# Selective scans on one core: diagonals of B read back from DRAM, softplus terms added by DMAs, the rate product made once

## The chip, the cores and the metric

The kernel runs on one core of a Trainium2 chip. A core has five engines, each with its own instruction stream: TensorE (PE in the profile, its weight loads PEld), VectorE (DVE), ScalarE (ACT), GpSimd (POOL) and SyncE (SP). SP, ACT and POOL can issue transfers (DMAs); all of them run on the core's 16 DMA engines. An engine executes its own stream in order. Engines wait for each other on semaphores, and an instruction that waits holds everything behind it on its engine.

The metric is the device time in microseconds of one execution. A difference under about 0.2% can't be told from no change for this kernel.

## The reference, cut to what matters

Layer 0 (group norm, triangle-style attention over a 256x256x128 map, residual) and the front of layer 1 (group norm, projection, 3x3 depthwise convolution, SiLU) are not touched by the change. What is touched is the selective scan of layer 1, which runs four times over L = 65,536 tokens: along rows, along columns, and both backwards.

```python
delta = softplus(dts + dt_bias)                    # (4, 256, L); dts is an 8-row product
def step(h, inp):                                  # h: (4, 256, 16), over l = 0..L-1
    d_t, x_t, B_t, C_t = inp
    dA = exp(d_t[..., None] * As)                  # decay of each of 16 states
    h = dA * h + (d_t * x_t)[..., None] * B_t[:, :, None, :]
    y = einsum('bkdn,bkn->bkd', h, C_t)            # sum over the 16 states
    return h, y
```

So for each of 4 directions, 256 channels and 16 states there is a recurrence over 65,536 tokens, with coefficient `exp(delta*A)` and input `delta*x*B`; its result is multiplied by C and summed over the 16 states.

## The kernel before, in words

The program goes through stages one after the other: group statistics, pair norm, attention, convolution, a transposing copy, the scans, the output. The scans take the stretch from about 4,700 to 27,660 us.

**Tiles and order of a scan.** Each direction is cut into 64 blocks of 1,024 tokens, so there are 4 x 64 = 256 blocks. The 256 channels are two halves h of 128 partitions, and there are 16 states m. One pair (m, h) is a step s of a block: s = 2m + h, 32 steps in a block. The order is written out by hand (a manual schedule): `body` goes through the steps, and for each step calls the functions below, some for a later step. A loop body covers 18 blocks.

In step s of a block:

- `recur` (L858): DVE's scan instruction runs the recurrence over 1,024 tokens, from the decay tile `da`, the input tile `mm` in PSUM and the `state`. After h = 1 a short reduce (L863) saves the last column, and POOL multiplies both halves of `hs` by the row of C (L865), two instructions.
- `turn` for step s+1: PE makes the next input `delta*x*B` in a PSUM tile `mm`, token tiles of 128 (8 of them, numbered j). `dxt` holds `delta*x` with tokens on the partitions. Half of the tiles (j = 0 to 3, DJ = 4) are a matrix product of `dxt` with a diagonal matrix `dg` whose diagonal is B (L846); each such product is two PE instructions in the profile. The other half are scaled first (`but`) and then transposed (L848), one PE instruction each. There are two `mm` tiles, and everything that makes a PSUM tile of this kind (turn, rate, turn_rate) takes them in turn.
- `collect_some`: PE adds transposes of finished `hs` tiles to the output in PSUM (L617), up to 10 in a step, less in a few steps (`share`).
- `decay` for step s+4: ACT makes `da` = exp(delta*A) (L839).
- `scale` for step s+6: ACT makes the diagonals `dg`, each the identity times a column of B (L833), and the scaled tiles `but` (L835), two of each in a step.
- `fetch` (L826), after h = 1: SP loads the row of C, spread to all partitions (`cc`, 512 KB), for state m+4. Its tile comes free when POOL's multiplications of state m are done, so SP waits there.

In steps 6 and 8 the previous block's output is added to `yb` by DVE (L898), stored, and the next `yb` is loaded in step 16.

**The next block is prepared within the current one.** `begin` returns a list of pieces with a step each and a mark for before or after the scan of that step: (6) and (8) `rate`, an 8-row product plus bias in a `mm` tile (L750), and its absolute value on ACT (L759); (9) exp of minus that; (10) the logarithm of 1 + e (L766); (11) and (12) a rounding remainder w on ACT (L770, L774); (11) to (14) two additions of halves e and w to lw on POOL (L780, L777), so four POOL instructions; (18) and (20) `rate` once more, and `softplus` on DVE (L783), which takes the larger of the rate and zero, and adds lw; (22) and (24) `turn_rate`, which transposes delta on PE (L790), and `times_x` (L794), which multiplies it by x into `dxt` on DVE.

The lines that set the order:

```python
for m in range(4): fetch(blocks[0], m)     # SP, four rows of C ahead
...
recur(B, m, h)                             # DVE (and POOL after h = 1)
do(turn, u + 1)                            # PE
collect_some(...)                          # PE
if nxt: nxt.advance(s, True)               # pieces of the next block
do(decay, u + 4)                           # ACT
do(scale, u + 3 * NH)                      # ACT
if h == NH - 1 and ...: fetch(...)         # SP
```

Of the kernel before, what the change touches and what calls it, by code (L numbers as in the profile page):

```python
# [29 lines left out]
AF = mybir.ActivationFunctionType  # L30
ALU = mybir.AluOpType
# [4 lines left out]
P = 128  # L36
# [4 lines left out]
DI = 256  # L41
# [578 lines left out]
def scans(tc, io, c):  # L620
# [19 lines left out]
    with tc.tile_pool(name="e_w", bufs=1) as wp, tc.tile_pool(name="e_1", bufs=1) as sb1, tc.tile_pool(  # L640
# [14 lines left out]
        DJ = NJ // 2  # L655
# [10 lines left out]
        bus = ring("but", 4, [P, NJ - DJ, DI])  # L666
# [18 lines left out]
        class Block:  # L685
# [43 lines left out]

            def advance(self, now, after):  # L730
                if self.pieces is None:
                    self.pieces = begin(self)
                while self.pieces and self.pieces[0][:2] <= (now, after):
                    _, _, f, *args = self.pieces.pop(0)
                    f(*args)

        def begin(B):
# [20 lines left out]
            def size(h):  # L758
                nc.scalar.activation(B.e[:, h, :], B.pu[h], AF.Abs)  # L759

# [15 lines left out]
            def less(h):  # L776
                nc.gpsimd.tensor_tensor(B.lw[:, h, :], B.lw[:, h, :], B.w[:, h, :], ALU.add)  # L777

            def log1p(h):
                nc.gpsimd.tensor_tensor(B.lw[:, h, :], B.lw[:, h, :], B.e[:, h, :], ALU.add)  # L780

            def softplus(h):
                nc.vector.scalar_tensor_tensor(B.delta[:, h, :], B.pu[h], 0.0, B.lw[:, h, :], ALU.max, ALU.add)  # L783
# [8 lines left out]
            def times_x(i):  # L792
# [8 lines left out]
            return [  # L801
# [6 lines left out]
                (11, True, log1p, 0),  # L808
                (11, True, one_plus),
                (12, True, log1p, 1),  # L810
                (12, True, rest),
                (13, True, less, 0),
                (14, True, less, 1),

                (18, False, rate, 0),
                (18, True, softplus, 0),
                (20, False, rate, 1),
                (20, True, softplus, 1),
# [4 lines left out]
            ]  # L823
# [3 lines left out]

        def scale(B, m, h):  # L830
            dg, bu = dgs[m % 4], bus[m % 4]
            for j in range(h * DJ // 2, (h + 1) * DJ // 2):
                nc.scalar.activation(dg[:, j, :], c.ident, AF.Copy, scale=B.bt[:, B.slot(j), m : m + 1])  # L833
                at = B.slot(DJ + j)
                nc.scalar.activation(bu[:, j, :], B.dxt[:, DJ + j, :], AF.Copy, scale=B.bt[:, at, m : m + 1])  # L835

# [4 lines left out]
        def turn(B, m, h):  # L841
            d1 = B.d1 = mm()
            dg, bu = dgs[m % 4], bus[m % 4]
            hc = slice(h * P, (h + 1) * P)
            for j in range(DJ):
                nc.tensor.matmul(d1[:, j * P : (j + 1) * P], B.dxt[:, j, hc], dg[:, j, :], start=True, stop=True)  # L846
            for j in range(DJ, NJ):
                nc.tensor.transpose(d1[:, j * P : (j + 1) * P], bu[:, j - DJ, hc], c.ident)  # L848
            d1s.append(d1)
# [56 lines left out]
        share = {6: 0, 7: 8, 8: 0, 18: 3, 20: 3, 22: 5, 24: 5}  # L906

        def body(blocks, before, after):
# [16 lines left out]
            if before is None:  # L925
                blocks[0].load()
                blocks[0].load_tokens()
                blocks[0].advance(U, True)
                blocks[0].free = set(range(NJ // PB))
                blocks[1].load()  # L930
                for m in range(4):
                    fetch(blocks[0], m)
                for u in range(3 * NH):
                    do(scale, u)
                for u in range(4):
                    do(decay, u)
                do(turn, 0)
            for x, B in enumerate(blocks):
                nxt = at_hand.get(x + 1)
                for s in range(U):  # L940
# [22 lines left out]
                    do(scale, u + 3 * NH)  # L963
                    if h == NH - 1 and at(u + 1 + 3 * NH):
                        fetch(*at(u + 1 + 3 * NH)[:2])
# [32 lines left out]
def output(tc, io, c):  # L998
# [75 lines left out]
    "y": (NT, DI),  # L1074
}
# [58 lines left out]
```

## Time and profile before

| | |
|---|---|
| time, median of 3 | 28,445.06 us (28,438.65 to 28,445.41) |
| span of the profiled execution | 28,447.5 us |
| PE busy | 26,610.1 us (94%) |
| ACT busy | 25,332.4 us (89%) |
| DVE busy | 24,922.2 us (88%) |
| POOL busy | 22,944.4 us (81%) |
| DMA, mean over the span | 128 GB/s |
| granted TensorE clock, mean | 0.965 |

The profiled execution is given by its span, from its first to its last instruction; it is 2.4 us above the median of the timed runs, under 0.01%.

How it is read: a group line names a line of the kernel, engine, operation, output and inputs, and then busy time, the mean of one instruction, and the idle time of the engine before it with what ended it. A timeline line gives the start in us, how long the merged instructions took, engine, line, operation and count, and in brackets idle time before it and its releaser. A window line gives a stretch, its length, the busy time of PE, PEld, DVE, ACT and POOL (with counts), the granted PE clock (1.00 is full), the DMA engines' busy share and the GB/s. Most of the program is one repeated block, so the block is what has to be read, in order of time.

### The profile page before, as it was taken

How to read it: one execution, taken by the hardware profiler on the slowest of the kernel's cores; microseconds unless marked ns; L12 is line 12 of the kernel's file. 1: busy time of each engine (PE TensorE's matmuls, PEld its weight loads, DVE VectorE, ACT ScalarE, POOL GpSimd, SP SyncE). 2: the span in 40 equal slices, each digit the busy share in tenths (PEclk: the TensorE clock that was granted, in tenths of full speed). 3: DMA queues.
4: the chain of work that ended last, by engine and by line, in shares of the span. 5: the costliest groups of instructions: out<-in, count | busy, mean ns of one | idle time of the engine just before them, and what ended most of it. 6: DMA issues, size and time to landing. Idle time of an engine off the chain costs nothing. (4 is left out here: it accounts for less than half of the span.)

```text
span 28447.5 us, 528099 instructions
## 1 busy us (share of the span) xinstructions
PE 26610.1 (94%) x196490; PEld 22529.2 (79%) x196490; DVE 24922.2 (88%) x24253; ACT 25332.4 (89%) x49673; POOL 22944.4 (81%) x10118
## 2 busy tenths in 40 slices
PE   8999996999999999999999999999999999999998
PEld 3555444888888888888888888888888888888884
DVE  4777665999999999999999999999999999999987
ACT  6875224999999999999999999999999999999987
POOL 2443002999999999999999999999999999999983
PEclk9999998999999999999999999999999999999999
DMA  5112345433433333333334333333333333333335
GB/s 206 55 50 71 111 116 115 132 132 129 133 130 133 132 131 132 132 131 132 128 132 133 131 133 132 131 132 129 132 132 130 133 132 129 132 130 132 133 132 172
DMA packets 1923996, 3630.07 MB, mean 128 GB/s; under 512 B 532297, under 2 KB 1240009, under 8 KB 1889490
## 3 DMA queue, kind: packets, MB, share of 16 engines
q1 hardware_dynamic: 1424722, 3339.77, 34.6%
q10 hardware_dynamic: 496640, 255.88, 3.2%
q8 instruction: 1568, 25.69, 0.4%
q14 instruction: 1066, 8.73, 0.1%
HBM read 3002.42 MB, written 592.84 MB: 126 GB/s over the span
## 5 line engine op out<-in xcount | busy, mean ns | idle before, releaser
L865 POOL TENSOR_TENSOR hs<-hs,cc 128x1024 f32<-128x1024 f32 x8192 | 19202.5, 2380 | 1346.1 <-DVE state L863 679.9
L858 DVE TENSOR_TENSOR_SCAN hs<-da,state,mm 128x1024 f32<-128x1024 f32 x8192 | 18976.6, 2340 | 1465.4 <-PE mm L848 1074.7
L846 PE MATMUL mm<-dg,dxt 128*128 128x128 f32 x65536 | 9305.0, 287 | 1065.1 <-DVE hs L858 886.1
L846 PEld LDWEIGHTS mm<-dg,dxt 128*128 128x128 f32 x65536 | 8328.4, 199 | 2257.9 <-DVE hs L858 1897.8
L839 ACT ACTIVATE da<-delta,A 128x1024 f32<-128x1024 f32 x8192 | 9328.4, 1139 | 112.2 <-PEq L984 76.0
L617 PE MATMUL y<-ident,hs 128*128 128x128 f32 x65536 | 8511.4, 275 | 1.4 <-POOL hs L865 1.4
L835 ACT ACTIVATE but<-dxt,bt 128x256 f32<-128x256 f32 x16384 | 8150.2, 497 | 11.4 <-DVE dxt L794 11.4
L617 PEld LDWEIGHTS y<-ident,hs 128*128 128x128 f32 x65536 | 7494.1, 143 | 1.9 <-POOL hs L865 1.9
L833 ACT ACTIVATE dg<-ident,bt 128x128 f32<-128x128 f32 x16384 | 6393.1, 390 | 0.2
L848 PE MATMUL mm<-ident,but 128*128 128x128 f32 x32768 | 5092.5, 280 | 0.0
L848 PEld LDWEIGHTS mm<-ident,but 128*128 128x128 f32 x32768 | 4011.4, 146 | 0.0
L750 PE MATMUL mm<-dt,dtw 9*128 9x512 f32 x4096 | 2033.0, 615 | 265.9 <-DMA bt<-mid_bk 184.5
L385 POOL TENSOR_TENSOR an<-ex,rs 128x1024 f32<-128x1024 f32 x512 | 970.2, 1895 | 1024.5 <-PE tp L394 566.3
L780 POOL TENSOR_TENSOR lw<-lw,e 128x1024 f32<-128x1024 f32 x512 | 1207.7, 2384 | 336.3 <-ACT lw L766 336.3
L750 PEld LDWEIGHTS mm<-dt,dtw 9*128 9x128 f32 x4096 | 680.7, 184 | 959.5 <-issue 733.3
L500 POOL MEMSET pad<- 128x10 f32 x32 | 3.7, 117 | 1650.0 <-PE ps L537 1639.9
L777 POOL TENSOR_TENSOR lw<-lw,w 128x1024 f32<-128x1024 f32 x512 | 1202.9, 2375 | 0.0
L537 PE MATMUL ps<-pad,w 128*128 128x512 f32 x2048 | 954.8, 610 | 161.0 <-ACT xi L525 161.0
L372 ACT ACTIVATE ex<-sc,nm 128x256 f32<-128x256 f32 x2048 | 1013.7, 499 | 0.4
L759 ACT ACTIVATE e<-mm 128x1024 f32<-128x1024 f32 x512 | 524.7, 1025 | 522.1 <-PE mm L750 521.9
L355 DVE CUSTOM_DVE_ANT_0 sc<-ps,bias 128x256 f32<-128x256 f32 x2048 | 746.2, 421 | 117.3 <-PE ps L340 117.3
L394 PEld LDWEIGHTS tp<-ident,an 128*128 128x128 f32 x4096 | 467.5, 141 | 470.7 <-POOL an L385 235.1
(137 smaller groups left out, 18522.4 us busy)
## 6 DMA issues: line engine op xcount, KB each, us to landing
cc<-mid_dc SPq DMA_DIRECT2D x2048, 512.0 KB
cc<-mid_dcT SPq DMA_DIRECT2D x2048, 512.0 KB
xk<-mid_xk SPq DMA_DIRECT2D x256, 1024.0 KB
yb<-mid_y SPq DMA_DIRECT2D x256, 1024.0 KB
mid_y<-yb SPq DMA_DIRECT2D x256, 1024.0 KB
xt<-mid_xT SPq DMA_DIRECT2D x64, 1024.0 KB
mid_xk<-xk ACTq DMA_DIRECT2D x32, 2048.0 KB
mid_y<-y ACTq DMA_DIRECT2D x32, 2048.0 KB
```

The source lines that it names most:

```text
L372: nc.scalar.activation(exs[u][:, x, :], scs[u][:, e, jt, :], AF.Exp, scale=-1.0, bias=nms[u][:, e, jt : jt + 1], accum_out=sms[u][:, x : x ...
L617: nc.tensor.matmul(out, in_, c.ident, is_transpose=True, start=start, stop=stop, skip_group_check=True)
L750: nc.tensor.matmul(pu[:, q : q + T], dtw[0 : DR + 1, k, h * P : (h + 1) * P], B.dt[0 : DR + 1, q : q + T], start=True, stop=True,)
L777: nc.gpsimd.tensor_tensor(B.lw[:, h, :], B.lw[:, h, :], B.w[:, h, :], ALU.add)
L780: nc.gpsimd.tensor_tensor(B.lw[:, h, :], B.lw[:, h, :], B.e[:, h, :], ALU.add)
L833: nc.scalar.activation(dg[:, j, :], c.ident, AF.Copy, scale=B.bt[:, B.slot(j), m : m + 1])
L835: nc.scalar.activation(bu[:, j, :], B.dxt[:, DJ + j, :], AF.Copy, scale=B.bt[:, at, m : m + 1])
L839: nc.scalar.activation(da, B.delta[:, h, :], AF.Exp, scale=A[:, B.S.k * NH + h, m : m + 1])
L846: nc.tensor.matmul(d1[:, j * P : (j + 1) * P], B.dxt[:, j, hc], dg[:, j, :], start=True, stop=True)
L848: nc.tensor.transpose(d1[:, j * P : (j + 1) * P], bu[:, j - DJ, hc], c.ident)
L858: nc.vector.tensor_tensor_scan(o, d0, d1, state[:, m, h : h + 1], ALU.mult, ALU.add)
L865: nc.gpsimd.tensor_tensor(hs[:, x, :], hs[:, x, :], ccs[m % 4], ALU.mult)
```

## The change

Three edits in the scans; the rest is unchanged.

1. Of eight token tiles three (j = 0, 2, 4) instead of four go through a diagonal. ACT no longer makes the diagonals. Instead, per block, four times (one for each 4 states) ACT copies the columns of B into a zeroed tile `z` with a spacing of 128 (`spread`), SP writes `z` (128 x 1,664, 852 KB) to DRAM, and for each state SP reads back a skewed view of it (`diagonal`, 128 rows of 1,536 bytes, 197 KB): row p starts p elements earlier in its row of `z`, so the spaced values land on a diagonal. Five tiles (j = 1, 3, 5, 6, 7) go through `but`.
2. The softplus sum is made in place: ACT writes max(rate, 0) into delta (Relu) beside the absolute value, and POOL issues three DMAs that add lw, e and w (1 MB each) to delta in SBUF, at the pieces (12), (15) and (18). POOL's four additions and DVE's two are gone.
3. With that, `rate` is made once per half (steps 6 and 8); steps 18 and 20 collect 10 transposes as others do.

```diff
-        DJ = NJ // 2
+        DJ = 3
+        BJ = NJ - DJ
+        by_diagonal, by_scale = (0, 2, 4), (1, 3, 5, 6, 7)
+        GS = 4
+        ZL = P * (GS * DJ + 1)
...
+        zs = ring("z", 1, [P, ZL])
+        for z in zs:
+            nc.vector.memset(z, 0.0)
...
+            def apart(self, g):
+                return io["apart"][self.b % 2, g]
...
             def size(h):
                 nc.scalar.activation(B.e[:, h, :], B.pu[h], AF.Abs)
+                nc.scalar.activation(B.delta[:, h, :], B.pu[h], AF.Relu)
...
-            def less(h):
-                nc.gpsimd.tensor_tensor(B.lw[:, h, :], B.lw[:, h, :], B.w[:, h, :], ALU.add)
-
-            def log1p(h):
-                nc.gpsimd.tensor_tensor(B.lw[:, h, :], B.lw[:, h, :], B.e[:, h, :], ALU.add)
-
-            def softplus(h):
-                nc.vector.scalar_tensor_tensor(B.delta[:, h, :], B.pu[h], 0.0, B.lw[:, h, :], ALU.max, ALU.add)
+            def add(name):
+                nc.gpsimd.dma_start(out=B.delta, in_=getattr(B, name), accum_op=ALU.add)
...
+            def spread(g):
+                z = zs[0]
+                first, step = B.slot(by_diagonal[0]), B.slot(by_diagonal[1]) - B.slot(by_diagonal[0])
+                nc.scalar.copy(
+                    z[:, P - 1 : P - 1 + GS * DJ * P].rearrange("p (m j q) -> p j m q", j=DJ, q=P)[:, :, :, 0],
+                    B.bt[:, first : first + step * (DJ - 1) + 1 : step, g * GS : (g + 1) * GS],
+                )
+                nc.sync.dma_start(out=B.apart(g), in_=z)
+
+            pieces = [(10 + 3 * g, True, spread, g) for g in range(DS // GS)]
+            return sorted(pieces + [
                 (6, False, rate, 0),
                 (6, True, size, 0),
                 (8, False, rate, 1),
                 (8, True, size, 1),
                 (9, True, exp),
                 (10, True, log),
-                (11, True, log1p, 0),
                 (11, True, one_plus),
-                (12, True, log1p, 1),
                 (12, True, rest),
-                (13, True, less, 0),
-                (14, True, less, 1),
-
-                (18, False, rate, 0),
-                (18, True, softplus, 0),
-                (20, False, rate, 1),
-                (20, True, softplus, 1),
+                (12, True, add, "lw"),
+                (15, True, add, "e"),
+                (18, True, add, "w"),
                 (22, False, turn_rate, 0),
                 (22, True, times_x, 0),
                 (24, False, turn_rate, 1),
                 (24, True, times_x, 1),
-            ]
+            ], key=lambda x: x[:2])
...
+        def diagonal(B, m):
+            of = B.apart(m // GS)
+            of = bass.AP(of.tensor, of.offset + P - 1 + m % GS * DJ * P, ((ZL - 1, P), (1, DJ * P)))
+            nc.sync.dma_start(out=dgs[m % 4].rearrange("p j q -> p (j q)"), in_=of)
...
         def scale(B, m, h):
-            dg, bu = dgs[m % 4], bus[m % 4]
-            for j in range(h * DJ // 2, (h + 1) * DJ // 2):
-                nc.scalar.activation(dg[:, j, :], c.ident, AF.Copy, scale=B.bt[:, B.slot(j), m : m + 1])
-                at = B.slot(DJ + j)
-                nc.scalar.activation(bu[:, j, :], B.dxt[:, DJ + j, :], AF.Copy, scale=B.bt[:, at, m : m + 1])
+            bu = bus[m % 4]
+            for x in range(h * BJ // 2, (h + 1) * BJ // 2):
+                j = by_scale[x]
+                nc.scalar.activation(bu[:, x, :], B.dxt[:, j, :], AF.Copy, scale=B.bt[:, B.slot(j), m : m + 1])
...
-            for j in range(DJ):
-                nc.tensor.matmul(d1[:, j * P : (j + 1) * P], B.dxt[:, j, hc], dg[:, j, :], start=True, stop=True)
-            for j in range(DJ, NJ):
-                nc.tensor.transpose(d1[:, j * P : (j + 1) * P], bu[:, j - DJ, hc], c.ident)
+            for x, j in enumerate(by_diagonal):
+                nc.tensor.matmul(d1[:, j * P : (j + 1) * P], B.dxt[:, j, hc], dg[:, x, :], start=True, stop=True)
+            for x, j in enumerate(by_scale):
+                nc.tensor.transpose(d1[:, j * P : (j + 1) * P], bu[:, x, hc], c.ident)
...
-        share = {6: 0, 7: 8, 8: 0, 18: 3, 20: 3, 22: 5, 24: 5}
+        share = {6: 0, 7: 8, 8: 0, 22: 5, 24: 5}
...
+                for m in range(3):
+                    diagonal(blocks[0], m)
...
                     do(scale, u + 3 * NH)
+                    if h == 0 and at(u + 3 * NH):
+                        diagonal(*at(u + 3 * NH)[:2])
                     if h == NH - 1 and at(u + 1 + 3 * NH):
                         fetch(*at(u + 1 + 3 * NH)[:2])
...
+    "apart": (2, 4, P, P * 13),
```

In the streams of the changed kernel POOL's order is: both multiplications of state 5, the DMA for lw, those of states 6 and 7, the DMA for e, those of state 8, the DMA for w, those of state 9. The DMAs for e and w each wait for the one before to have landed, since all three write delta. On SP the read of a diagonal stands directly behind the load of C for the same state, and the writes of `z` stand between them at steps 10, 13, 16 and 19.

More of the change, by code (lines that the diff above doesn't have):

```diff
@@ L665, in scans @@
         dgs = ring("dg", 4, [P, DJ, P])
-        bus = ring("but", 4, [P, NJ - DJ, DI])
+        bus = ring("but", 4, [P, BJ, DI])
+        zs = ring("z", 1, [P, ZL])
+        for z in zs:
+            nc.vector.memset(z, 0.0)
         das = ring("da", DA, [P, TB])
@@ L799, in times_x @@
                 )
-            return [
+            def spread(g):
[8 more added lines that the diff above has]
+            return sorted(pieces + [
                 (6, False, rate, 0),
```

## The prediction

> **What bounds the kernel now.** I read the page's groups first, then one block in the timeline, engine by engine, then short windows for DMA and clock. The scan group carries the program: 8,192 scans of DVE at 2.34 us, as many multiplications on POOL at 2.38.
>
> ```profile
> L865 POOL TENSOR_TENSOR hs<-hs,cc 128x1024 f32<-128x1024 f32 x8192 | 19202.5, 2380 | 1346.1 <-DVE state L863 679.9
> L858 DVE TENSOR_TENSOR_SCAN hs<-da,state,mm 128x1024 f32<-128x1024 f32 x8192 | 18976.6, 2340 | 1465.4 <-PE mm L848 1074.7
> L780 POOL TENSOR_TENSOR lw<-lw,e 128x1024 f32<-128x1024 f32 x512 | 1207.7, 2384 | 336.3 <-ACT lw L766 336.3
> ```
>
> The SP timeline shows the period: yb is loaded (L948) at 15021.78, 15110.66 and 15199.09, so a block takes 88.4 to 88.9 us. DVE's timeline says where it goes.
>
> ```profile
> 15100.90 2.35 DVE L858 TENSOR_TENSOR_SCAN hs<-da,state,mm 128x1024 f32<-128x1024 f32 x1
> 15103.17 1.23 DVE L783 SCALAR_TENSOR_TENSOR delta<-mm,lw 128x1024 f32<-128x1024 f32 x1
> 15106.22 2.35 DVE L858 TENSOR_TENSOR_SCAN hs<-da,state,mm 128x1024 f32<-128x1024 f32 x1 [1.82 <-PE mm L848]
> ...
> 15111.30 1.23 DVE L783 SCALAR_TENSOR_TENSOR delta<-mm,lw 128x1024 f32<-128x1024 f32 x1 [0.28 <-PE mm L750]
> 15112.83 2.35 DVE L858 TENSOR_TENSOR_SCAN hs<-da,state,mm 128x1024 f32<-128x1024 f32 x1 [0.30 <-PE mm L848]
> ...
> 15115.29 2.35 DVE L858 TENSOR_TENSOR_SCAN hs<-da,state,mm 128x1024 f32<-128x1024 f32 x1
> 15117.55 1.20 DVE L794 TENSOR_TENSOR dxt<-mm,xk 128x1024 f32<-128x1024 f32 x1
> 15119.39 2.35 DVE L858 TENSOR_TENSOR_SCAN hs<-da,state,mm 128x1024 f32<-128x1024 f32 x1 [0.64 <-PE mm L848]
> ...
> 15128.45 4.58 DVE L858 TENSOR_TENSOR_SCAN hs<-da,state,mm 128x1024 f32<-128x1024 f32 x2
> 15133.07 0.16 DVE L863 TENSOR_REDUCE state<-hs 128x2 f32<-128x2 f32 x1
> 15133.17 4.58 DVE L858 TENSOR_TENSOR_SCAN hs<-da,state,mm 128x1024 f32<-128x1024 f32 x2
> ```
>
> An undisturbed pair of steps takes 15133.17 - 15128.45 = 4.72 us, all of it DVE: DVE bounds such stretches, and nothing taken from ACT or PE there shortens them. Sixteen pairs are 75.6 us; the other 13 are three interruptions: steps 18 to 21 (second rate, softplus) last 14.39 instead of 9.45, steps 22 to 25 (times_x) 13.16, steps 6 to 9 (output) 13.2.
>
> **What goes.** (a) Steps 18 to 21 become plain: -4.94 us a block. With the second rates go two softplus of 1.23 and the late turns behind them. (b) A turn has 3x2 + 5 = 11 PE instructions instead of 12. PE starts one every 0.11 us (L846 at 15049.90, eight, L848 at 15050.80). Only the four turns that DVE waits for (0.64 twice, 0.61 and 0.58 after the output) turn this into time: -0.44. (c) DVE's short waits for ACT ("0.16 <-ACT da", at 15095.98 and similar): -0.3. Together -5.7 us a block, over 256 blocks -1,460. POOL's four additions (9.5 us a block) go too; they bring nothing by themselves, since POOL's lag ends in tiles that are collected three states later.
>
> **What is added beside other work.** ACT, per block, by starts in its timeline: the 64 diagonals at 0.29 go (-18.6), 16 `but` at 0.40 come (+6.4), two Relus priced as the Abs of 1.03 (+2.1), four spreads at no more than a `dg` of 0.39 (+1.6): 86.8 busy becomes about 78, hidden under DVE's 83. Each us beyond that cover would cost 256. A spread waits until the last write of `z` has landed; the decays behind it run up to four steps ahead, so I price it at nothing. SP gets four writes and sixteen reads at 0.33 to 0.38 of issue, some 7 us on a queue that mostly waits. The mm tile is held one Relu longer at steps 6 and 8, while DVE is busy with output. The memset of `z` runs once.
>
> **What lands on the path: three adding DMAs in a row.** The trace of before has no such DMA. Let g be what POOL spends to issue one, and D the time from there to its landing. POOL's place in the block is in the profile: it finishes state 5 at 15091.28 and starts what stands there now.
>
> ```profile
> 15081.87 9.45 POOL L865 TENSOR_TENSOR hs<-hs,cc 128x1024 f32<-128x1024 f32 x4 [1.91 <-DVE state L863]
> 15091.28 4.73 POOL L780 TENSOR_TENSOR lw<-lw,e 128x1024 f32<-128x1024 f32 x2
> ```
>
> So lw's DMA starts at 15091.28. Behind it two states are multiplied (4.73 each): e's starts at 15100.74 + g. One state more, 4.73, is shorter than D, so POOL then waits for e to land, and w's starts at 15100.74 + 2g + D and lands at 15100.74 + 3g + 2D. It is needed by turn_rate at step 22. In this block step 10 starts at 15081.59 (by the DVE timeline), so without the interruption step 22 starts 12 steps, 28.4 us, later, at 15109.97. The eight transposes take 0.95 and would hide until that scan ends after 2.27; 1.3 us of slack put the limit at 15111.3. The stall is S = 2D + 3g - 10.5 us a block. PE stands at turn_rate, so the next turn, the collecting transposes and the next scan stand behind it; POOL's wait holds the multiplications of state 9, on which SP's next load of C and the diagonal behind it depend.
>
> The bounds of g: 0.33 (SP's issue of cc, L826) and 2.4 (a whole POOL instruction of L865); the nearest row is ACT's issue, 0.395 at L577, so 0.4. The bounds of D come from DMA windows.
>
> ```profile
> 15049.99 0.33 SPq L826 DMA_DIRECT2D cc<-mid_dc  x1
> ...
> 15050.00:15051.00 1.00, 1.00 (x11) 1.00 (x10) 1.00 (x1) 1.00 (x3) 1.00 (x1) 1.00 0.10 16
> 15051.00:15052.00 1.00, 1.00 (x12) 1.00 (x10) 1.00 (x2) 1.00 (x4) 1.00 (x1) 1.00 0.83 274
> ...
> 15066.00:15067.00 1.00, 0.91 (x9) 0.89 (x8) 1.00 (x1) 1.00 (x3) 1.00 (x2) 1.00 1.00 389
> ...
> 15104.00:15106.00 2.00, 2.00 (x11) 2.00 (x11) 0.40 (x1) 2.00 (x5) 2.00 (x2) 0.50 0.00 0
> ```
>
> A load starts to move about 1.05 us after its issue, and full engines move 389 GB/s. Low: 1 MB as one undisturbed copy, 1.05 + 2.7 = 3.75. An add must fetch delta as well as its term, so I double the transfer: 1.05 + 5.4 = 6.5 undisturbed. High: it gets half of the engines, 1.05 + 10.8 = 11.9. The SP queue is not idle there: the mean DMA share of the block is 0.40 before, and `z` (852 KB at steps 13, 16, 19), yb and the diagonals fall into these very steps. I take 8.5, a little nearer to the undisturbed add than to half of the engines. S = 17 + 1.2 - 10.5 = 7.7.
>
> After such a stop PE is slow. In the last window above the granted clock is 0.50, and there L846 and L848 take 1.96 + 1.06 us instead of 1.06 + 0.60: about +1.4 us before the next scan, which I add to a stall above 3 us. Per block -5.7 + 7.7 + 1.4 = +3.4, in 256 blocks +870. The first block, made with nothing beside it, pays its chain once, +15. 28,447.5 + 885 = 29,330; I say 29,350. The profiled execution is 2.4 us above the median, which changes nothing.
>
> The Trainium skill has a rule that speaks against the change. "Collectives: The Full Stack", Part 3, says that an add in the DMA datapath runs at half of a copy because it needs two source reads (no run here shows it yet); with it D is 6.5 before contention and the sum would be -0.6 us a block (-150 in all), without it D is 3.75, the stall is nothing and the sum is -1,460. "DMA: Bandwidth & Descriptors", Anatomy of one DMA, gives about 2.0 us + bytes/436e3 for a transfer issued from GpSimd, 4.4 us for 1 MB; by that estimate, too, the sum ends near 27,000.
>
> **The rivals.** (1) *The adds land in time: faster.* If an add costs little more than a copy, D = 3.75 to 5.2, S is at most 1.1 and the gain is 4.6 to 5.7 us a block: 26,990 to 27,270; at D = 6.2 (S = 3.1, before the clock's part) still 27,780. The point that decides: S plus the clock's 1.4 equals 5.7 at D = 6.8. For it: 389 GB/s in the windows, and engines idle 60% of the block. Against it: two dependent landings after 15100.74 with 10.6 us to go, and POOL cannot issue earlier. (2) *The diagonals come late.* Before, ACT made them six steps ahead and POOL's lag did not matter. Now SP reads them behind a load of C that waits for POOL: state m ends on POOL 5.1 us after its last scan (the load at 15086.62, against a last scan that ends before 15081.5), so the diagonal of m+4 is issued 0.8 us into step 2m+4 and PE may need it three scans later; with the slack within a scan the lead is 7.0. Beside cc alone it needs 1.05 + 1.6 + 0.5 = 3.2; behind a `z` write (2.2) 5.4; with an add taking every second turn 5 more, 3.4 too late. Three states a block meet an add: +10 a block without S, 28,447 + 256 x 4.5 = 29,600. Against it: the stall S itself gives the reads time. (3) *An add is slower than a doubled copy.* At D = 11.9, e too is late: three landings and issues after 15091.28, 15091.28 + 36.9 - 15111.3 = 16.9, with clock 18.3, less 5.7: +12.6, 31,670. (4) *Nothing to see*: gain and stall cancel around D = 6.8; a narrow strip.
>
> **How the numbers follow.** The chain of adds with D from 6.9 to 11: 0.42, times 28,500 to 31,000. Rival 2: 0.12; rival 3: 0.09; rival 1: 0.33; rival 4: 0.04. Slower by over 0.2%, about what measurement tells apart here: 0.42 + 0.12 + 0.09 = 0.63; faster 0.33; same 0.04. The likeliest case's own range is 28,500 to 31,000. The range for 8 in 10 takes in rival 1 and leaves out the end of rival 3: 26,950 to 31,300.
>
> **What the profile after would show.** L783 and the second L750 gone, L846's successor at 49,152 and L848's at 40,960 instructions, ACT near 78 us a block, no softplus between steps 18 and 21. Right: each block has one long PE and DVE gap before turn_rate, released by the DMA into delta, DVE idle of 8 to 9 us there with a clock of 0.50 after it, POOL waiting at the second or third DMA. Wrong: no wait for delta (then rival 1, block about 83 us), or PE's waits for `dg` spread over many states (rival 2). What breaks the prediction most easily is D: each us of it moves the time by 512.

## The result, and the profile after

The changed kernel takes 31,991.13 us, median of 4 runs (31,958.28 to 32,035.75), against 28,445.24 for the kernel before (28,438.65 to 28,445.6). The ratio is 1.1248, with a 95% interval of 1.1232 to 1.1264: 3,546 us slower, 13.9 us in each of the 256 blocks. The profiled execution spans 32,034.0 us with a mean granted clock of 0.903 (0.965 before).

The groups of the changed kernel (line, engine, operation, count, then busy time, mean ns of one, idle time before it and what ended most of it):

```profile
L871 DVE TENSOR_TENSOR_SCAN hs<-da,state,mm 128x1024 f32<-128x1024 f32 x8192 | 18930.7, 2339 | 4535.8 <-PE mm L861 3729.3
L859 PE MATMUL mm<-dg,dxt 128*128 128x128 f32 x49152 | 8109.8, 307 | 3782.9 <-DMA dg<-mid_apart 2860.5
L809 ACT COPY z<-bt 128x12 f32<-128x12 f32 x1024 | 212.0, 207 | 2494.5 <-DMA mid_apart<-z 2494.5
L788 POOL DMA_DIRECT2D delta<-w x256 | 224.4, 877 | 2017.9 <-DMA delta<-e 951.5
L799 DVE TENSOR_TENSOR dxt<-mm,xk 128x1024 f32<-128x1024 f32 x512 | 620.7, 1212 | 1204.3 <-PE mm L795 1194.3
L795 PE MATMUL mm<-ident,delta 128*128 128x128 f32 x4096 | 734.9, 339 | 963.2 <-DMA delta<-w 963.2
```

The scans take what they took (2,339 ns each), so DVE's idle time is the account. Before the scans it was 1,465.4 us and is 4,535.8; before times_x it was 2.3 and is 1,204.3. The two softplus of each block, 624.2 us of DVE and 116.4 of waiting for them, are gone (both lines are of the kernel before):

```profile
L783 DVE SCALAR_TENSOR_TENSOR delta<-mm,lw 128x1024 f32<-128x1024 f32 x512 | 624.2, 1219 | 116.4 <-PE mm L750 89.5 <-POOL lw L777 25.7
L794 DVE TENSOR_TENSOR dxt<-mm,xk 128x1024 f32<-128x1024 f32 x512 | 613.8, 1199 | 2.3 <-PE mm L790 2.3
```

3,070.4 + 1,202.0 - 740.6 = +3,532, of the 3,546 that were measured. PE is the one DVE waits for, and PE stands at two places: 2,860.5 us at diagonals that have not been read back, 963.2 us at delta, whose third add has not landed.

Both are to be seen in one block of the changed kernel. The timeline of PE, where it waits longest between steps 12 and 22, and that of POOL, which issues the adds:

```profile
15078.54 1.62 PE L859 MATMUL mm<-dg,dxt 128*128 128x128 f32 x6 [4.45 <-DMA dg<-mid_apart]
...
15094.33 1.62 PE L859 MATMUL mm<-dg,dxt 128*128 128x128 f32 x6 [4.83 <-DMA dg<-mid_apart]
...
15102.63 1.94 PE L795 MATMUL mm<-ident,delta 128*128 128x128 f32 x8 [3.90 <-DMA delta<-w]
...
15066.72 0.89 POOL L788 DMA_DIRECT2D delta<-lw  x1
15078.51 0.89 POOL L788 DMA_DIRECT2D delta<-e  x1 [1.54 <-DMA delta<-lw]
15092.57 0.89 POOL L788 DMA_DIRECT2D delta<-w  x1 [8.46 <-DMA delta<-e]
```

From lw's issue at 15066.72 to the first use of delta at 15102.63 pass 36 us. The same 36 us in windows (length; busy PE, PEld, DVE, ACT, POOL; PE clock, DMA share, GB/s):

```profile
15066.70:15078.50 11.80, 7.22 (x64) 6.78 (x62) 9.25 (x6) 11.64 (x20) 10.28 (x6) 0.92 0.99 267
15078.50:15092.60 14.10, 10.96 (x76) 10.76 (x76) 9.54 (x6) 6.13 (x11) 5.63 (x4) 0.82 1.04 304
15092.60:15103.50 10.90, 5.27 (x23) 4.93 (x24) 2.35 (x1) 9.71 (x18) 10.17 (x5) 0.55 1.01 303
```

The DMA engines are full throughout (0.99 to 1.04), moving 267 to 304 GB/s, though their mean share between 10,000 and 26,000 us is 0.67; the granted clock falls to 0.55 as PE stops. The reads that PE waited for at 15078.54 and 15094.33 stand in SP's timeline (reads go out in the order of the states; these are for states 9 and 11):

```profile
15067.26 0.38 SPq L840 DMA_DIRECT2D dg<-mid_apart  x1
...
15081.01 4.74 SPq L840 DMA_DIRECT2D dg<-mid_apart  x1
```

PE stood ready for the first at 15074.09, 6.8 us after its issue, and got it after 11.3. POOL had finished state 5, which frees the tile of C ahead of this read, at 15066.79, 5.1 us after that state's last scan; that is its lag in the kernel before. So POOL did not make this read late: it went out on time, and took long on full engines. The second went out 4.0 us after POOL had finished state 7 (15076.98), behind a load of yb and a write of `z`, took 4.74 us to issue and was used 13.3 us after it.

The DMA queues of the changed kernel (packets, MB, share of 16 engines) and its DMA issues (KB each, median us from issue to landing) give the sizes:

```profile
q1 hardware_dynamic: 2162002, 5017.82, 46.7%
q0 software_dynamic: 110592, 805.36, 12.1%
...
delta<-lw POOLq DMA_DIRECT2D x256, 1024.0 KB, 11.3
delta<-e POOLq DMA_DIRECT2D x256, 1024.0 KB, 13.0
delta<-w POOLq DMA_DIRECT2D x256, 1024.0 KB, 10.5
```

q0 holds the adds alone: 12.1% of 32,034 us over 768 adds is 5.05 us of all engines for one. q1's copies need 46.7% x 32,034 / 5,017.82 = 2.98 us per MB, 3.13 for an add's 1.05 MB. So an add costs 1.6 times what the kernel's other transfers need per byte (their packets are smaller, 2.3 KB on average against 7.3), and 1.9 times the 2.7 us that the same bytes take at the 389 GB/s of full engines in the kernel before. It lands 10.5 to 13.0 us after its issue.

After the result there were three theories. Theory C: the chain of three dependent landings is most of the loss. Theory P: the diagonals are late because SP holds their reads behind a load of C, which waits for POOL. Theory Q: the DMA engines are full between steps 12 and 22, and everything is late in its queue. Below, a time without an interval is that of one execution, beside the kernel before on the same chip.

### The profile page after: what moved, and what is told of

The parts are those of the page before. It is cut to its first block, busy times and chain, and to the rows that moved or that the text cites. A ratio compares the mean times of both kernels' runs of the same rounds, so it can differ in the third digit from the quotient of the medians.

```text
span 32034.0 us, 509251 instructions
## 1 busy us (share of the span) xinstructions
PE 26619.2 (83%) x186250; PEld 22762.3 (71%) x186250; DVE 24360.5 (76%) x23742; ACT 23193.7 (72%) x38921; POOL 21251.3 (66%) x9862
## 3 DMA queue, kind: packets, MB, share of 16 engines
q1 hardware_dynamic: 2162002, 5017.82, 46.7%
q0 software_dynamic: 110592, 805.36, 12.1%
## 5 line engine op out<-in xcount | busy, mean ns | idle before, releaser
L871 DVE TENSOR_TENSOR_SCAN hs<-da,state,mm 128x1024 f32<-128x1024 f32 x8192 | 18930.7, 2339 | 4535.8 <-PE mm L861 3729.3
L859 PE MATMUL mm<-dg,dxt 128*128 128x128 f32 x49152 | 8109.8, 307 | 3782.9 <-DMA dg<-mid_apart 2860.5
L859 PEld LDWEIGHTS mm<-dg,dxt 128*128 128x128 f32 x49152 | 6879.4, 212 | 4997.7 <-issue 2877.6
L848 ACT ACTIVATE but<-dxt,bt 128x256 f32<-128x256 f32 x20480 | 8974.3, 496 | 95.7 <-PE mm L861 83.1
L617 PEld LDWEIGHTS y<-ident,hs 128*128 128x128 f32 x65536 | 7983.8, 149 | 2.5 <-POOL hs L878 2.5
L861 PE MATMUL mm<-ident,but 128*128 128x128 f32 x40960 | 6429.1, 292 | 0.0
L861 PEld LDWEIGHTS mm<-ident,but 128*128 128x128 f32 x40960 | 5319.4, 154 | 0.0
L809 ACT COPY z<-bt 128x12 f32<-128x12 f32 x1024 | 212.0, 207 | 2494.5 <-DMA mid_apart<-z 2494.5
L788 POOL DMA_DIRECT2D delta<-w x256 | 224.4, 877 | 2017.9 <-DMA delta<-e 951.5
L799 DVE TENSOR_TENSOR dxt<-mm,xk 128x1024 f32<-128x1024 f32 x512 | 620.7, 1212 | 1204.3 <-PE mm L795 1194.3
L795 PE MATMUL mm<-ident,delta 128*128 128x128 f32 x4096 | 734.9, 339 | 963.2 <-DMA delta<-w 963.2
L795 PEld LDWEIGHTS mm<-ident,delta 128*128 128x128 f32 x4096 | 609.3, 177 | 1041.7 <-issue 1037.7
L760 PE MATMUL mm<-dt,dtw 9*128 9x512 f32 x2048 | 1081.6, 649 | 184.4 <-DMA bt<-mid_bk 183.3
## 6 DMA issues: line engine op xcount, KB each, us to landing
delta<-lw POOLq DMA_DIRECT2D x256, 1024.0 KB, 11.3
delta<-w POOLq DMA_DIRECT2D x256, 1024.0 KB, 10.5
```

Of the source, the lines that this page charges most:

```text
L617: nc.tensor.matmul(out, in_, c.ident, is_transpose=True, start=start, stop=stop, skip_group_check=True)
L760: nc.tensor.matmul(pu[:, q : q + T], dtw[0 : DR + 1, k, h * P : (h + 1) * P], B.dt[0 : DR + 1, q : q + T], start=True, stop=True,)
L795: nc.tensor.transpose(B.pt[:, j, h * P : (h + 1) * P], B.delta[:, h, at : at + P], c.ident)
L848: nc.scalar.activation(bu[:, x, :], B.dxt[:, j, :], AF.Copy, scale=B.bt[:, B.slot(j), m : m + 1])
L861: nc.tensor.transpose(d1[:, j * P : (j + 1) * P], bu[:, x, hc], c.ident)
L871: nc.vector.tensor_tensor_scan(o, d0, d1, state[:, m, h : h + 1], ALU.mult, ALU.add)
```

## The experiments

**1. The adds without the diagonals** (edits 2 and 3 alone; the diagonals made by ACT, four of eight tiles, as before).

```diff
+                nc.scalar.activation(B.delta[:, h, :], B.pu[h], AF.Relu)
...
+            def add(name):
+                nc.gpsimd.dma_start(out=B.delta, in_=getattr(B, name), accum_op=ALU.add)
...
-                (18, False, rate, 0),
-                (18, True, softplus, 0),
-                (20, False, rate, 1),
-                (20, True, softplus, 1),
+                (12, True, add, "lw"),
+                (15, True, add, "e"),
+                (18, True, add, "w"),
```

> The adding DMAs and the single rate product alone; the diagonals are made by ACT as before, four of eight tiles. Theory Q (the adds, the writes of z and the rest fill the DMA engines between steps 12 and 22, and most of the loss is the diagonals that come late in the SP queue): no diagonal is read, so only a stop before turn_rate is left and the adds land sooner, 7 to 10 us instead of 10.5 to 13; 28,300 to 29,400. Theory C (the chain of three dependent landings is most of the loss by itself): the stop stays 15 us or more, 31,000 or above.

Measured: 30,101.37 beside 28,444.29, +1,657. Neither theory named it: the chain alone is slower than before, but it is less than half of the loss. Groups and landings of this run:

```profile
L847 DVE TENSOR_TENSOR_SCAN hs<-da,state,mm 128x1024 f32<-128x1024 f32 x8192 | 18979.1, 2340 | 1504.3 <-PE mm L837 685.7
L785 PE MATMUL mm<-ident,delta 128*128 128x128 f32 x4096 | 762.8, 349 | 2303.7 <-DMA delta<-w 2303.7
...
delta<-lw POOLq DMA_DIRECT2D x256, 1024.0 KB, 9.5
delta<-e POOLq DMA_DIRECT2D x256, 1024.0 KB, 11.1
delta<-w POOLq DMA_DIRECT2D x256, 1024.0 KB, 7.4
```

One stop a block, 2,303.7 / 256 = 9.0 us, at turn_rate, and nowhere else. Without z and diagonals beside them the landings are 1.8 to 3.1 us shorter. The idle time before the scans is 1,504.3, no less than the 1,465.4 of before.

**2. The diagonals without the adds** (edit 1 alone; rate twice, sums on POOL and DVE as before).

> The diagonals from DRAM alone (three of eight tiles); softplus as before, with two rates, four additions on POOL and two on DVE. Theory Q: the engines are busy some 60% without the adds, the diagonals come in time, 28,000 to 28,500. Theory P (the diagonals are late because SP holds them behind the load of C, which waits for POOL): POOL's four additions put it 9.6 us behind, the diagonals of some two states are 5 to 7 us late in each block, 29,700 or above.

Measured: 31,113.81, +2,670, more than the adds cost alone. Theory P named it (29,700 or more), theory Q did not. Two groups, and one stop in DVE's timeline:

```profile
L870 PE MATMUL mm<-dg,dxt 128*128 128x128 f32 x49152 | 7755.3, 297 | 3719.0 <-DMA dg<-mid_apart 2826.7
L814 ACT COPY z<-bt 128x12 f32<-128x12 f32 x1024 | 207.2, 202 | 3374.5 <-DMA mid_apart<-z 3374.3
```

```profile
15070.71 2.35 DVE L882 TENSOR_TENSOR_SCAN hs<-da,state,mm 128x1024 f32<-128x1024 f32 x1 [10.16 <-PE mm L872]
```

The windows ahead of that stop show why full engines alone are not the cause:

```profile
15052.00:15058.00 6.00, 6.00 (x39) 4.52 (x39) 5.56 (x4) 2.42 (x5) 6.00 (x4) 1.00 0.00 0
15058.00:15064.00 6.00, 0.23 (x3) 0.00 (x0) 2.50 (x2) 0.00 (x0) 6.00 (x4) 0.91 0.81 241
15064.00:15070.00 6.00, 2.08 (x10) 2.12 (x11) 0.00 (x0) 2.62 (x6) 6.00 (x3) 0.50 1.03 413
```

For 6 us the DMA engines are empty (0.00) while POOL is busy: its four additions to lw (9.5 us) stand ahead of the multiplications that free a tile of C, so these come late, SP waits, and the reads behind it are not even issued. The read that ends this stop is

```profile
15058.84 0.69 SPq L851 DMA_DIRECT2D dg<-mid_apart  x1
```

PE had begun to wait at 15058.24, before this issue, and POOL had finished state 7 only 14.3 us after that state's last scan (15057.03 against 15042.70). Then the reads come at once, the engines are full (1.03), and PE waits. Here it is POOL's lag that makes the read late, as theory P has it, and not the engines alone, as in the block of the changed kernel above.

**3. The whole change, but nobody waits for the adds.** The three DMAs add lw to e, w and e instead of to delta, so the bytes are the same; delta is then max(rate, 0) alone.

```diff
-                nc.gpsimd.dma_start(out=B.delta, in_=getattr(B, name), accum_op=ALU.add)
+                nc.gpsimd.dma_start(out={"lw": B.e, "e": B.w, "w": B.e}[name], in_=B.lw, accum_op=ALU.add)
```

> The changed kernel, but the three DMAs add lw into e, w and e again, where nobody waits for them (delta is left at max(rate, 0), so the log terms of softplus are left out). The traffic is the same, no engine waits for a landing before turn_rate or on POOL. Theory C and theory P: without these waits nothing is late, about 27,000 to 27,400. Theory Q: the engines are as full as before, PE's stops for diagonals stay at 2 to 3 of some 4 us a block, 29,300 to 30,500.

Measured: 31,718.25. Only 273 us come back, so the wait for delta is not what holds the changed kernel as a whole. No theory named this: C and P had 27,000 to 27,400, and Q 29,300 to 30,500. The adds now leave closer together, within 15.2 us in one block (15015.17, 15025.08, 15030.32) against 25.9 in the changed kernel. PE's wait for diagonals grows from 2,860.5 to 3,883.1 us:

```profile
L859 PE MATMUL mm<-dg,dxt 128*128 128x128 f32 x49152 | 7950.1, 302 | 4918.2 <-DMA dg<-mid_apart 3883.1
```

POOL waits for no add here and makes no additions, and still the reads are late. That speaks against theory P as the cause in the changed kernel, and for full engines (1.00 to 1.08 from 15,020 to 15,045 us of this run); how much of it comes from the adds standing closer together was not tested.

**4. The whole change, the diagonal of m+4 read ahead of the load of C of m+4**, some 4.7 us sooner.

```diff
-                    if h == 0 and at(u + 3 * NH):
-                        diagonal(*at(u + 3 * NH)[:2])
                     if h == NH - 1 and at(u + 1 + 3 * NH):
+                        diagonal(*at(u + 1 + 3 * NH)[:2])
                         fetch(*at(u + 1 + 3 * NH)[:2])
```

> The changed kernel, but SP issues the diagonal of state m+4 ahead of the load of C of m+4 instead of behind it, which gives the read two steps (4.7 us) more of lead with the same traffic. Theory C: 31,500 to 32,000, as changed. Theories Q and P: PE's stops for diagonals (2,860 us in all) fall to a third or less, 29,500 to 30,700; what is left is the stop before turn_rate.

Measured: 31,348.06, 643 us less than the change, between what C (31,500 and more) and what Q and P (30,700 and less) had said. It is the mirror of run 3:

```profile
L859 PE MATMUL mm<-dg,dxt 128*128 128x128 f32 x49152 | 7753.9, 297 | 1373.5 <-DVE hs L871 533.4
L795 PE MATMUL mm<-ident,delta 128*128 128x128 f32 x4096 | 762.6, 348 | 3777.8 <-DMA delta<-w 3777.8
```

With the diagonals mostly in time, the wait for delta rises from 963.2 to 3,777.8. So the two stops hide each other: in runs 1 and 2 they cost 1,657 and 2,670, together 3,546 and not 4,327, and whichever is taken away, the other takes its place. That is why neither run 3 nor run 4 gains much.

**5. The diagonals alone, with a ring of six tiles**, read for m+6 (ahead of the load for m+4).

```diff
-        dgs = ring("dg", 4, [P, DJ, P])
+        dgs = ring("dg", 6, [P, DJ, P])
...
-                    if h == 0 and at(u + 3 * NH):
-                        diagonal(*at(u + 3 * NH)[:2])
+                    if h == NH - 1 and at(u + 11):
+                        diagonal(*at(u + 11)[:2])
```

> The diagonals from DRAM alone, as in the run before, but in a ring of six tiles, read for state m+6 ahead of the load of C of m+4: six steps more of lead (14 us), same traffic, same lag of POOL. Theory P (SP holds the diagonals behind the load of C, which waits for POOL): with more lead than POOL's lag of 9.6 us PE's stops for diagonals go, 28,000 to 28,900; the rest above 28,000 would be ACT waiting for the last write of z. Theory Q (the engines are too full for the writes of z and the diagonals): stays above 30,000.

Measured: 29,272.53, above theory P's range (28,900) and 1,841 less than run 2: the lead, not the volume, was most of the diagonals' price there. What is left has another releaser:

```profile
L882 DVE TENSOR_TENSOR_SCAN hs<-da,state,mm 128x1024 f32<-128x1024 f32 x8192 | 18948.2, 2339 | 2195.1 <-ACT da L863 1121.3
```

DVE now waits 1,121.3 us for decays that stand on ACT behind a spread, which stands there until the last write of `z` has landed (2,350.5 us of waiting between 10,000 and 26,000 us):

```profile
ACT z L814 <- DMA mid_apart<-z: 2350.5, 181, 17.5
```

**6. The same, and only B's values are written.** The rows in DRAM are zeroed once before the scans, and three DMAs a block put B's columns into them as single floats; ACT's spread and the tile `z` are gone from the loop.

```diff
+            def spread(x):
+                j, of = by_diagonal[x], io["apart"][B.b % 2]
+                nc.sync.dma_start(
+                    out=bass.AP(of.tensor, of.offset + P - 1 + x * P, ((ZW, P), (DJ * P, DS), (1, 1))),
+                    in_=B.bt[:, B.slot(j), :].unsqueeze(2),
+                )
+            pieces = [(10 + x, True, spread, x) for x in range(DJ)]
```

> As diag_early, but the spaced rows in DRAM are zeroed once, and per block only the values of B are written into them, three DMAs of 128 x 16 single floats instead of four of 852 KB; ACT's copies into z and its waits for z are gone. If the writes of z cost something through ACT's waits or the traffic, 300 to 1,000 us less than diag_early, 27,900 to 28,300. If single floats are slow to write, equal or more.

Measured: 28,254.12. The rest of the diagonals' price is gone, 1,018 us of it with the writes of `z`. Timed:

> The diagonals alone, read six states ahead from rows of which only B's values are written, timed against the kernel before: 28,254 in one look. Both theories: 28,150 to 28,350, faster than before by 0.4 to 1%.

28,244.75 against 28,437.52, ratio 0.9931 (0.9915 to 0.9948): diagonals read back from DRAM are a small gain once they have their lead.

**7. On top of run 6, rate once, and the sums on engines**: max(rate, 0) by ACT into delta, POOL's four additions into lw as before, and DVE adds lw to delta.

```diff
+                nc.scalar.activation(B.delta[:, h, :], B.pu[h], AF.Relu)
...
-                nc.vector.scalar_tensor_tensor(B.delta[:, h, :], B.pu[h], 0.0, B.lw[:, h, :], ALU.max, ALU.add)
+                nc.vector.tensor_tensor(B.delta[:, h, :], B.delta[:, h, :], B.lw[:, h, :], ALU.add)
```

> As diag_early_sparse, and the rate product made once: ACT leaves max(rate, 0) in delta as in the changed kernel, POOL adds e and w to lw as before, DVE adds lw to delta (two of 1.2 us) in steps 18 and 20. No adding DMA. The steps 18 to 21 should take 9.45 + 2.4 instead of 14.4 us, the block 85 to 86 us, bound by DVE and POOL together (POOL 85.3): 27,500 to 28,000. If DVE's sums of two SBUF tiles get in POOL's way, up to 28,400.

Measured: 29,336.91, ratio 1.0314 (1.0296 to 1.0331); a miss. The group says why:

```profile
L798 DVE TENSOR_TENSOR delta<-delta,lw 128x1024 f32<-128x1024 f32 x512 | 2009.2, 3924 | 68.1 <-POOL lw L792 59.0
```

The addition with both inputs in SBUF takes 3,924 ns, where the softplus of the same size with one input in PSUM took 1,219. 512 x 2.7 = 1,380 us more of DVE, which is the bound; 1,083 were lost against run 6.

**8. The whole change with the diagonals of run 6.**

> The changed kernel with the diagonals early and the sparse writes; the three adding DMAs stay. No stop for diagonals and no write of z is left, so what remains above 27,000 is the chain of adds alone at the traffic of before plus the diagonals: landings of 8 to 11 us, a stop of 8 to 12 us before turn_rate, 29,200 to 30,300. If the adds are slow only because of the z writes, 28,000 or below.

Measured: 31,567.97; a miss of more than 1,000 us. With the diagonals out of the way, the chain of adds alone still costs most of the loss, 3,125 of 3,546 us:

```profile
L799 PE MATMUL mm<-ident,delta 128*128 128x128 f32 x4096 | 762.3, 348 | 4366.1 <-DMA delta<-w 4366.1
```

One block of it, POOL's issues and PE's wait:

```profile
15081.00 0.87 POOL L792 DMA_DIRECT2D delta<-lw  x1
15094.16 0.88 POOL L792 DMA_DIRECT2D delta<-e  x1 [2.87 <-DMA delta<-lw]
15108.65 0.88 POOL L792 DMA_DIRECT2D delta<-w  x1 [8.86 <-DMA delta<-e]
...
15118.53 1.94 PE L799 MATMUL mm<-ident,delta 128*128 128x128 f32 x8 [18.81 <-DMA delta<-w]
```

37.5 us from the first issue to the last landing, of which PE waits 18.8. The stop is 17 us a block on average, against 9 in run 1: the landings are longer (13.9, 12.6 and 9.2 against 9.5, 11.1 and 7.4). In this block the single floats of run 6 are written beside lw's add (from 15,081.00 to 15,094.20 us the engines are at 0.92 and move 136 GB/s); that this is why it lands later was not tested. If nothing else is wrong, the chain simply starts some 18 us too late; the last runs test that.

**9. The chain begun seven steps sooner**: rates at steps 1 and 3, Exp and Ln at 4 and 5, the adds at 5, 11 and 17; turn_rate stays at 22 and 24.

```diff
-                (6, False, rate, 0),
+                (1, False, rate, 0),
...
-                (12, True, add, "lw"),
-                (15, True, add, "e"),
-                (18, True, add, "w"),
...
+                (5, True, add, "lw"),
...
+                (11, True, add, "e"),
+                (17, True, add, "w"),
```

> All three edits, diagonals read six states ahead from rows of which only B's values are written, and the chain of the three adds begun seven steps sooner: the rates at steps 1 and 3 instead of 6 and 8, Exp and Ln at 4 and 5, the adds at 5, 11 and 17, turn_rate left at 22 and 24. In the kernel with the three adds at 12, 15 and 18 and the same diagonals PE waited 4,366.1 us in all for the last landing (18 us in each of the 256 blocks), and its chain took 37.5 us from the first issue. Theory C (the chain of landings is what is left, and it is too late by 18 us, not too long): seven steps are 7 x 2.6 = 18 us, the stop goes, and the time is 31,568 - 4,366 = 27,200, between 26,900 and 27,900. Theory Q (the adds load the DMA engines whatever their place, and the time comes back as late reads of C or of diagonals): over 28,600.

Measured: 29,929.57, ratio 1.0522 (1.0505 to 1.0540). 1,638 us came back, not 4,366. The time lies where theory Q had it (over 28,600), but PE waits for no read between 10,000 and 26,000 us; it still waits for the third add. POOL's timeline, and PE's wait in the same block:

```profile
15006.31 0.90 POOL L792 DMA_DIRECT2D delta<-e  x1
15020.95 1.19 POOL L792 DMA_DIRECT2D delta<-w  x1
...
15033.50 1.94 PE L799 MATMUL mm<-ident,delta 128*128 128x128 f32 x8 [8.46 <-DMA delta<-w]
```

The third add leaves 14.6 us after the second, which lands in 9.4 (median): its place in POOL's stream, behind the multiplications of three states, holds it now, not the landing before it. The chain's start had moved by seven steps, its third add by one (18 to 17). It needs 12.5 us itself, and 8.46 are missing.

**10. The same start of the chain with ACT's diagonals of before.**

> The diagonals made on ACT as before, the product of rates made once, three adds, and the chain begun seven steps sooner as in the run beside it. The same kernel with the adds at 12, 15 and 18 took 30,101 with 2,303.7 us of PE's waiting for the last landing. C: that wait goes, 30,101 - 2,304 = 27,800, and less if the clock comes back too (27,200 to 28,000); ACT, 86% busy there, becomes the bound. Q: over 28,600.

Measured: 29,403.37, a miss for theory C. The number is again one that theory Q had (over 28,600), and again not for Q's reason: no diagonal is read in this run, PE's waits for loads of C are 18.0 us between 10,000 and 26,000 us, and its waits for the third add there are 1,145.2, 6.7 in each of 172 blocks:

```profile
PE mm L785 <- DMA delta<-w: 1145.2, 172, 8.3
```

**11. The chain without gaps**: rates at steps 0 and 2, the adds at 4, 8 and 12, with the diagonals of run 6.

```diff
-                (5, True, add, "lw"),
+                (4, True, add, "lw"),
...
-                (11, True, add, "e"),
-                (17, True, add, "w"),
+                (8, True, add, "e"),
+                (12, True, add, "w"),
```

> As the kernel with the chain seven steps sooner, with the chain tightened: rates at steps 0 and 2, Exp and Ln at 3 and 4, the adds at 4, 8 and 12 (they were at 5, 11 and 17, and POOL, which runs some 5 us behind DVE, issued the third at 15,020.95, 14.6 us after the second at 15,006.31, though the second had landed after 9.4). There PE still waited 8.5 us in each block for the third landing. C: the third add now leaves as the second lands, 8 us or more before the former place, the wait goes, and the time is 29,930 - 256 x 8.5 = 27,750, between 27,300 and 28,200: the change's three edits then beat the kernel before. Q: the reads of C and of the diagonals come late instead, over 28,900.

Measured: 27,621.48 against 28,439.64, ratio 0.9712 (0.9696 to 0.9728). All three edits of the change are in it, and it beats the kernel before by 818 us. POOL's issues, and turn_rate of that block:

```profile
15053.40 0.88 POOL L792 DMA_DIRECT2D delta<-lw  x1 [0.61 <-ACT lw L781]
...
15063.88 0.90 POOL L792 DMA_DIRECT2D delta<-e  x1 [0.20 <-issue]
...
15074.04 1.01 POOL L792 DMA_DIRECT2D delta<-w  x1
...
15092.66 1.09 PE L799 MATMUL mm<-ident,delta 128*128 128x128 f32 x8
```

The third add is issued 18.6 us before turn_rate and takes 9.4 (median of this run): PE waits for no landing here. The load has not gone; from 15,050 to 15,080 us, where the adds are, the engines are at 0.63, 0.90 and 1.05. The last two windows:

```profile
15060.00:15070.00 10.00, 8.29 (x71) 7.89 (x72) 9.93 (x9) 10.00 (x17) 9.80 (x6) 1.00 0.90 234
15070.00:15080.00 10.00, 10.00 (x92) 9.83 (x90) 9.93 (x7) 10.00 (x18) 10.00 (x6) 1.00 1.05 257
```

Theory Q in its last form, that the load brings the time back as late reads whatever the place of the adds, falls with this run. What stays of it is the changed kernel's own block, where the reads had a lead of 6.8 us and took 11.

## Why the prediction was wrong

**The direction was right, the size was not:** +905 was forecast, +3,546 measured, beyond the range's 31,300. Two steps failed: the sum has no term for late diagonals, which took 11.2 us of PE's time a block, and D, the landing of an add, was 10.5 to 13.0 us and not 8.5. By the prediction's own steps:

- **The term that failed in size is D, 8.5 us.** The measured landings in the changed kernel are 11.3, 13.0 and 10.5, and an issue took 0.88 and not 0.4. Put into the same working: lw leaves at 15091.28, e at 15102.6, w at 15115.6, and delta is ready at 15126.1, 14.8 after the limit of 15111.3. -5.7 + 14.8 + 1.4 is +10.5 a block, about 31,150. That this is near the measured time is luck, since the changed kernel stops 3.8 us a block at delta and not 14.8. Without the late diagonals the working holds: with the landings of run 1 it gives 8.8, and 9.0 were recorded; with those of run 8 it gives 15.7, and 17.1 were. The choice "a little nearer to the undisturbed add than to half of the engines" is what went wrong; the bound of 11.9 was too low as well. Doubling the copy for an add was near (5.4 against 5.05 us of engine time). What was missing is that the change itself fills the engines just there: their windows are at 0.99 to 1.04.
- **"I price it at nothing"**, of the spread behind the landing of `z`, was wrong: ACT waits 2,494.5 us there, and runs 5 and 6 differ by 1,018 us, the price of these waits and writes when nothing else covers them. SP's issues of "0.33 to 0.38" were not always that either: one read of a diagonal took up to 6.75 us to issue (L840, median 0.38).
- **The wrong argument stood in rival 2**, "the stall S itself gives the reads time". Measured, PE waits 11.2 us a block at diagonals (2,860.5 / 256) and 3.8 at delta (963.2 / 256, where S was 7.7). The diagonals are late first, and it is their stops that give the adds time. The waits stand at about three reads a block (446 in 153 blocks between 10,000 and 26,000 us; in the block shown states 3, 9 and 11), the number that rival 2 had, though only the last two stand beside adds and the first behind the load of the next x. Its working holds too: it gave a read 7.0 us of lead, 10.4 to land beside `z` and an add, and +10 us a block; the read for state 9 had 6.8, took 11.3, and the whole was 11.2. It had 0.12, and should have been added to the chain and not set against it. That run 2 also lost 10.4 a block is luck: it has no adds, its reads are late by POOL's lag, and 4.0 of the 10.4 went with the writes of `z` (run 6).
- **Rival 3's 31,670** is within 321 us, which is luck: it is a stop of 16.9 us at delta, and the changed kernel has 3.8 there. The case that it describes is run 8, with no late diagonals: landings of 11.9 on average, a stop of 17.1 and 31,568 us.
- **What goes, -5.7 a block, was too much as it stands.** The softplus (740.6 us, 2.9 a block, with its waits) went. The other 2.8, waits that were to vanish, hardly did: 1,504.3 us are left before the scans in run 1 (some of it the slow restart after its stop), and 1,362.3 in run 11 against 1,465.4. There the rates stand at steps 0 and 2, and new waits came: 526.4 us for PE's collecting transposes and 361.1 for ACT's Relu before the scans. Run 11's 818 us is little more than half of the 1,460 that were summed.
- **Right:** 49,152 and 40,960 PE instructions, ACT at 79 us a block between 10,000 and 26,000 us (12,084.7 us in 153 blocks; 78 was said), POOL's waits at the second and third add, the clock near 0.5 after a stop, and that D moves the time most.

The rule in the Trainium skill, "Collectives: The Full Stack", Part 3, that an add in the DMA datapath runs at half of a copy, is of the right kind: the rows above say 1.6 to 1.9 copies, by what a copy is taken to be. The estimate from "DMA: Bandwidth & Descriptors", Anatomy of one DMA, 4.4 us for 1 MB, is not what these rows show: the shortest median landing of an add in any of the runs is 7.4 (run 1), and in the changed kernel they are 10.5 to 13.0; the measurement decides. No run has an add with the engines to itself.

What stays open: how the 818 us of run 11 divide between its edits. The diagonals alone gave 193; whether the rest is all from the softplus was not taken apart.

## What to carry to other kernels

Before pricing a transfer on the path, add up what the change puts into the same microseconds: a mean DMA share of 0.4 says nothing of a stretch that the change fills itself. Two stops that hide each other look as if neither mattered when each is removed alone, so price each with the other gone, and add a second mechanism to the first unless it needs the other's absence. A chain of dependent DMAs is paid by its place: here the same adds cost 4,366 us of waiting at steps 12, 15 and 18 (run 8), and 33 us, all in one block, at 4, 8 and 12 (run 11), where each still took 9.4 to 10.8 us to land.

## What the runs showed that I had not expected

- A DVE addition of 128x1024 floats with both inputs in SBUF took a median of 3,340 ns (1,390 to 12,611, between 10,000 and 26,000 us) in run 7, with POOL 93% busy there; the softplus of the kernel before, with an input in PSUM, 1,219. The Trainium skill, "SBUF — State Buffer", Who interferes with whom, says why it may be so: a DVE instruction with two SBUF inputs contends with a GpSimd instruction that reads SBUF, and one with at most one does not, outside the two-port modes. The two numbers agree with it; DVE's addition with POOL idle was not tried.
- Writing single floats is cheap in bytes and not in engine time. In run 6, the window at the steps of these writes has the engines at 0.90 with only 100 GB/s:

```profile
15010.00:15020.00 10.00, 9.85 (x75) 8.20 (x73) 9.93 (x7) 10.00 (x16) 10.00 (x5) 1.00 0.90 100
```

- An add issued by POOL holds it 0.88 us (L788 above), more than twice SP's median of 0.33 to 0.38 for a load.
- Run 11 has the highest DMA share in the scans and the highest clock: 0.75 and 0.99 between 10,000 and 26,000 us, against 0.39 and 0.97 before. Busy DMA engines cost little there, since hardly anyone waits for them: all waits for a DMA in that stretch are POOL's and come to 135 us.
